# Last layer's expert results added in memory: tokens stored behind the attention, scatters that accumulate, rows copied from memory to the output

## The chip, the cores and the metric

The kernel runs on one core of one Trainium2 chip, in one launch. The metric is the time of one execution on the device in microseconds (us); of several executions the median is taken. Engines are called PE (matrix multiplication), DVE (vector), ACT (scalar), POOL (GpSimd) and SP (the engine that here only issues transfers). A view of the profile always belongs to one profiled execution.

## The reference

The input `x` has 16 x 256 tokens of 128 channels, all in float32. Four residual layers follow one another, each on a layer norm of `x`:

```python
x = x + attn_a(layernorm(x))      # 16 heads of 8, in blocks of 64 tokens of a sequence
x = x + ffn(layernorm(x))         # mixture of experts
x = x + attn_b(layernorm(x))      # 16 heads, over the 16 sequences, with a bias
x = x + ffn(layernorm(x))         # the same experts and the same router weights
```

The mixture of experts chooses two of eight experts for every token:

```python
logits = flat_x @ Wr
top_vals, top_idx = top_k(logits, 2)
rw = softmax(top_vals)
h  = silu(flat_x @ Wg[e]) * (flat_x @ Wu[e])         # hidden size 512
out = sum over the two experts e of  rw_e * (h @ Wd[e]) / sqrt(12)
```

So every one of the 4096 tokens gets two expert rows, and the final output is the token after `attn_b` plus these two rows.

## The kernel before

The tokens stay on the chip in four tiles `xq[q]`, one for each quarter of the 256 positions: 128 partitions x 8 groups x 128 channels, 1024 tokens a quarter.

**Experts by lists of tiles.** A router (`router(layer, q)`) finds each token's two experts and scatters the token's normalised row twice into a memory tensor `sorted_in[layer]`, where every expert has a region. A row there carries the 128 channels, its weight in column C, and in column C + 1 the place where its result is to go. `tile_tables` then cuts the regions into tiles of 256 rows: 39 tiles a layer, in three lists of 9, 8 and 22. The first list is known after two quarters, the second after three, the third after all four. An expert tile is two *units* of work in `experts(layer)`: its rows (`xin`, L861) and its expert's weights (`w`, three loads of 256 KB, L877 to L879) are fetched by SP two tiles ahead into three buffers; PE multiplies by `wg` and `wu` (L947), ACT and DVE form `h` (L952 to L955), PE multiplies by `wd` (L897) and turns the result back (L908), and ACT scales it into `yo` (L913; six buffers). Then POOL scatters the 256 rows by two indirect DMAs of 128 rows each (L920) into `results[layer]`, to the places in `to`. Where the last list's tiles overlap rows done before, `to` points to padding rows behind the results.

**Combination.** `results[layer]` has two rows for every token, so all scatters of a layer go to different rows and are not ordered among each other. `combine(layer, part)` loads the pairs of half a quarter (`back`, L973, 512 KB), waiting for the scatters of all tiles that can hold rows of that quarter (`READY`: 24, 24, 31 and 39 tiles), and DVE adds the two rows to `xq` (L983). In layer 1 two further DMAs store the half quarter from `xq` to the output (L986).

**Order of the work.** The program text sets the order: `weave` takes steps of one generator between those of another. Layer 0's expert tiles run beside `attn_b` of the quarters before; `begin_b(q)` combines layer 0's results for quarter q and prepares its attention, `finish_b(q)` multiplies by the output weights and adds to `xq[q]` (L580). After the third quarter's `finish_b`, `begin_b` of the fourth runs beside the first four tiles of layer 1. The layer's first tiles run beside the attention and the router of the fourth quarter; the rest run alone, up to `BEGIN[q]` units, each time followed by the combination of a quarter. Every engine works through its own instructions in order, and SP's and POOL's DMA issues are part of that: an issue that waits holds up what stands behind it. Inside the framework an order of small pieces can be moved by its scheduler, so the order of each engine's instructions is read from the built program.

`declare_no_dep`, `add_to_no_dep_group` and `follow` tell the framework which accesses to a memory tensor are independent, and which waits are set by hand.

Of the kernel before, what the change touches and what calls it, by code (L numbers as in the profile page):

```python
# [64 lines left out]
K_PAD = K_DEST + TOP * NQ * NG  # L65
K_ROW = K_PAD + 2 * KMAX
K_FIRST = K_ROW + 2
K_END = K_FIRST + NE

B_Q, B_K, B_TOR, B_IQ, B_IK, B_IV = range(6)  # L70

# [1 line left out]
def _constants():  # L73
    p = np.arange(P)[:, None]
    h = np.arange(H)[None, :]
    c = np.zeros((P, K_END), np.float32)
    c[:, K_ID : K_ID + P] = np.eye(P)

    c[:, K_HM : K_HM + 4] = (p // D) % 4 == np.arange(4)[None, :]

    c[:, K_PM : K_PM + H] = p // 64 == h % 2
    c[:, K_M4 : K_M4 + H] = p // 32 == h % 4

    eye = np.eye(S)
# [19 lines left out]
    c[:, K_ROW : K_ROW + 2] = 2 * p + np.arange(2)  # L104

    c[:, K_FIRST : K_FIRST + NE] = NTOK * np.arange(NE)
    return c
# [3 lines left out]
def hybrid_kernel(  # L111
# [111 lines left out]
        nc.gpsimd.memset(t[:, 0:NG], 0.0)  # L223


    sorted_in = [dram.tile([NE * NTOK, RW], F32, name=f"sorted_in{i}") for i in range(2)]
    results = [dram.tile([TOP * NTOK + KMAX * TT, C], F32, name=f"results{i}") for i in range(2)]

    zero = const.tile([P, TT // P * RW], F32, name="zero")
    nc.gpsimd.memset(zero, 0.0)  # L230
# [354 lines left out]
    def router(layer, q):  # L585
# [12 lines left out]
        for g in range(NG):  # L598
# [253 lines left out]
    def experts(layer):  # L852
# [41 lines left out]
        def down(li, i, t, w, elsewhere, acc, pair, h):  # L894
# [7 lines left out]
            if pair == 1:  # L902
# [13 lines left out]
                    )  # L916
                to = p6.tile([P, 2], I32, tag="to", name=f"to_{n}")
                nc.vector.tensor_tensor(to, t[:, :, C + 1], elsewhere, ALU.max)
                for b in range(2):
                    put_row = nc.gpsimd.indirect_dma_start(  # L920
                        out=results[layer],
# [5 lines left out]
                    key = f"result_{layer}"  # L927
                    tc.declare_no_dep(put_row.ins, group=key, reason="rows of different places")
                    tc.add_to_no_dep_group(key, put_row.ins)
                    puts.setdefault(layer, []).append(put_row.ins)  # L930
# [35 lines left out]
        yield  # L966


    def combine(layer, part):
        q, gs = part // 2, slice(4 * (part % 2), 4 * (part % 2) + 4)  # L970
        rows_of = slice(part * 4 * P * TOP, (part + 1) * 4 * P * TOP)
        t = p2.tile([P, 4, TOP, C], F32, tag="back", name=f"back_{layer}_{part}")
        got = nc.sync.dma_start(  # L973
            out=t.rearrange("p g k c -> p g (k c)"),
            in_=results[layer][rows_of].rearrange("(g p k) c -> p g (k c)", p=P, k=TOP),
        )
        known = puts[layer][: 2 * READY[q]]
        key = f"result_{layer}"
        tc.declare_no_dep(got.ins, group=key, keep=known, reason="rows of tiles done before")
        tc.add_to_no_dep_group(key, got.ins)  # L980
        follow(got.ins, known)
        for k in range(TOP):
            nc.vector.tensor_tensor(xq[q][:, gs], xq[q][:, gs], t[:, :, k], ALU.add)  # L983
        if layer == 1:
            for s2 in range(2):
                nc.sync.dma_start(  # L986
                    out=out.rearrange("(g s) t c -> s t g c", s=2)[
                        s2, q * BS : (q + 1) * BS, gs
                    ],
                    in_=xq[q][s2 * BS : (s2 + 1) * BS, gs, :],  # L990
                )

# [34 lines left out]

    def begin_b(q):  # L1030
        for part in range(2 * q, 2 * q + 2):
            combine(0, part)
            yield
        yield from normal_b(q)
        yield from prepare_b(q, 0)
# [7 lines left out]
    for layer in range(2):  # L1043
# [10 lines left out]
        for q in range(NQ):  # L1054
            for half in range(2):
# [78 lines left out]
```

## Time and profile before

| | us |
|---|---|
| median of 3 runs | 983.16 |
| lowest and highest run | 980.27, 992.81 |
| the profiled execution | 1056.63 |
| its span, first to last instruction | 1054.9 |

| engine | busy us | share of the span |
|---|---|---|
| PE | 901.1 | 85% |
| DVE | 619.6 | 59% |
| ACT | 397.6 | 38% |
| POOL | 361.1 | 34% |

The profiled execution is longer than the timed ones, so shares of it are carried over rather than differences. The mean granted PE clock of it is 0.911.

How to read the lines: in a timeline, the columns are the start in us from the span's beginning, the duration in us, engine, line, operation, output <- inputs, the count, and in brackets how long the engine was idle before it and what ended that. In the chain of waits, each line is start, duration and what the end of the run was waiting for at that time. In a list of waits, it is who waited for whom, us in total, times, and the longest. In the groups of the page, it is line, engine, operation, output <- inputs, count, busy us, mean ns, and idle time before with what ended most of it.

### The profile page before, as it was taken

To read this page: it belongs to the slowest core of one execution; us is meant where nothing else is said; L and a number is where in the kernel's file an instruction comes from. 1 tells how busy PE (TensorE), PEld (TensorE's weight loads), DVE (VectorE), ACT (ScalarE), POOL (GpSimd) and SP (SyncE) were. 2 spreads that over 40 slices of the span, in tenths; PEclk is the share of its full clock that TensorE was granted. 3 is DMA by queue.
4 is the path that set the end of the run, shared out by engine and by line. 5 is a ranking of instruction groups with operands and counts; after the bars stand their busy time and mean duration, and the time that the engine had idled before them with its cause. 6 is when DMAs were issued, how large, how long until landed. Compare 5 with 4: busy or idle time off the path is not lost.

```text
span 1054.9 us, 17640 instructions
## 1 busy us (share of the span) xinstructions
PE 901.1 (85%) x5992; PEld 733.6 (70%) x5992; DVE 619.6 (59%) x1749; ACT 397.6 (38%) x773; POOL 361.1 (34%) x404
## 2 busy tenths in 40 slices
PE   5987897989989979989887789588976997999993
PEld 3765666768778758877765667467765776887872
DVE  4676357557746745577766447546754674456452
ACT  2442243244434323436444254233622332443431
POOL 2121522442443463341112631442225345333322
PEclk9997787689989999999997889898978988999997
DMA  7000000041333545673121211133203444568772
GB/s 198 3 2 1 29 14 1 21 127 41 99 101 106 151 149 166 196 225 96 42 81 41 65 58 42 61 95 127 81 14 109 121 134 148 170 192 253 222 213 88
DMA packets 104922, 107.69 MB, mean 102 GB/s; under 512 B 10688, under 2 KB 80320, under 8 KB 104832
## 3 DMA queue, kind: packets, MB, share of 16 engines
q1 hardware_dynamic: 95024, 87.36, 27.8%
q0 software_dynamic: 9088, 18.89, 5.1%
q8 instruction: 48, 0.79, 0.3%
q10 hardware_dynamic: 720, 0.30, 0.1%
q14 instruction: 42, 0.34, 0.1%
HBM read 83.38 MB, written 23.13 MB: 101 GB/s over the span
## 4 chain that ended last, share of the span: by engine, by line
PE 66%; DVE 12%; DMA 6%; another core or an unknown queue 5%; ACT 5%; issue 4%; POOL 1%; SPq 1%; ACTq 0%; POOLq 0%; DVEq 0%
PE g L947 11%; PE acc L897 10%; PE u L947 10%; PE o_A L441 6%; PE sc_A L411 6%; PE t_A L430 3%; PE v_B L354 3%; PE o_B L554 2%; DMA back<-results 2%; PE sc_B L517 2%; DMA xin<-sorted_in 2%; DMA results<-yo,to 2%; PE v_A L354 2%; PE lg_F L599 1%
## 5 line engine op out<-in xcount | busy, mean ns | idle before, releaser
L920 POOL DMA_INDIRECT results<-yo,to x156 | 154.1, 988 | 299.7 <-ACT yo L913 269.3
L897 PE MATMUL acc<-h,w 128*128 128x256 f32 x624 | 174.3, 401 | 12.1 <-DVE h L955 9.1
L947 PE MATMUL g<-xT,w 128*128 128x256 f32 x624 | 171.5, 394 | 4.4 <-issue 2.7
L947 PE MATMUL u<-xT,w 128*128 128x256 f32 x624 | 169.8, 393 | 3.8 <-DVE th L953 2.0
L952 ACT ACTIVATE th<-g 128x512 f32<-128x512 f32 x156 | 93.6, 600 | 203.8 <-PE g L947 132.1
L953 DVE SCALAR_TENSOR_TENSOR th<-th,g 128x512 f32<-128x512 f32 x156 | 106.4, 683 | 105.6 <-ACT th L952 84.0
L694 POOL DMA_INDIRECT sorted_in<-rows,pos_i_F x128 | 125.0, 977 | 124.7 <-issue 38.4
L897 PEld LDWEIGHTS acc<-h,w 128*128 128x128 f32 x624 | 121.6, 200 | 36.4 <-DVE h L955 14.8
L947 PEld LDWEIGHTS g<-xT,w 128*128 128x128 f32 x624 | 119.0, 198 | 23.0 <-issue 4.9
L947 PEld LDWEIGHTS u<-xT,w 128*128 128x128 f32 x624 | 115.7, 196 | 20.4 <-issue 3.4
L955 DVE TENSOR_TENSOR h<-th,u 128x512 f32<-128x512 f32 x156 | 106.6, 684 | 21.6 <-remote 5.6
L411 PE MATMUL sc_A<-k_A,q_A 128*128 128x256 f32 x256 | 86.4, 456 | 19.0 <-DVE ex_A L420 14.1
L441 PEld LDWEIGHTS o_A<-va,eT_A 128*64 128x64 f32 x1024 | 63.6, 147 | 20.4 <-issue 8.4
L411 PEld LDWEIGHTS sc_A<-k_A,q_A 128*128 128x128 f32 x256 | 50.8, 225 | 33.2 <-DVE ex_A L420 16.3
L441 PE MATMUL o_A<-va,eT_A 128*64 128x18 f32 x1024 | 67.7, 219 | 5.6 <-issue 3.1
L905 ACT COPY yT<-acc 128x256 f32<-128x256 f32 x78 | 29.0, 372 | 100.6 <-PE acc L897 89.2
L419 DVE TENSOR_REDUCE mx_A<-sc_A 128x8 f32<-128x512 f32 x64 | 43.1, 681 | 35.5 <-PE sc_A L411 34.8
L434 ACT COPY eT_A<-t_A 128x512 f32<-128x512 f32 x64 | 36.6, 589 | 67.9 <-PE t_A L430 61.8
L449 POOL TENSOR_TENSOR xq<-xq,att_A 128x128 f32<-128x128 f32 x32 | 14.6, 456 | 130.5 <-DVE att_A L373 120.1
L913 ACT ACTIVATE yo<-y,xin 128x128 f32<-128x128 f32 x156 | 48.6, 366 | 20.4 <-PE y L908 10.6
L425 ACT ACTIVATE ex_A<-ex_A 128x1024 f32<-128x1024 f32 x32 | 34.0, 1064 | 42.5 <-DVE ex_A L420 31.0
L430 PEld LDWEIGHTS t_A<-k_sb,ex_A 128*128 128x128 f32 x256 | 34.0, 159 | 20.7 <-issue 10.4
(173 smaller groups left out, 1318.0 us busy)
## 6 DMA issues: line engine op xcount, KB each, us to landing
w<-in_wg SPq DMA_DIRECT2D x78, 256.0 KB
w<-in_wu SPq DMA_DIRECT2D x78, 256.0 KB
w<-in_wd SPq DMA_DIRECT2D x78, 256.0 KB
xin<-sorted_in SPq DMA_DIRECT2D x78, 132.0 KB
back<-results SPq DMA_DIRECT2D x16, 512.0 KB
results<-yo,to POOLq DMA_INDIRECT x156
sorted_in<-zero SPq DMA_DIRECT2D x2, 1056.0 KB
sorted_in<-rows,pos_i_F POOLq DMA_INDIRECT x128
```

Source lines behind the costliest of these rows:

```text
L354: nc.tensor.matmul(pv[:, a * P : (a + 1) * P], lhsT=src[:, g * n + a].rearrange("p r k -> p (r k)"), rhs=w, start=True, stop=True,)
L411: nc.tensor.matmul(sc[:, v * 4 * BS : (v + 1) * 4 * BS], lhsT=qT[:, blk, 2 * v : 2 * v + 2, :].rearrange("p r k -> p (r k)"), rhs=kx[:, :, ...
L430: nc.tensor.transpose(pt[:, i * P : (i + 1) * P], ex[:, b, 2 * i : 2 * i + 2, :].rearrange("p h k -> p (h k)"), ident,)
L441: nc.tensor.matmul(po[b * BS : (b + 1) * BS, i * 18 : (i + 1) * 18], lhsT=eT[:, b, 2 * v + i % 2, u * BS : (u + 1) * BS], rhs=vt[:, b, 2 * ...
L694: put_row = nc.gpsimd.indirect_dma_start(out=sorted_in[layer], out_offset=bass.IndirectOffsetOnAxis(ap=pos_i[:, k, g : g + 1], axis=0), in ...
L897: nc.tensor.matmul(acc[:, 0:TT], lhsT=w[:, 2, hc * P : (hc + 1) * P], rhs=h[:, j * TT : (j + 1) * TT], start=(hc == 0), stop=(hc == NHC - 1),)
L913: nc.scalar.activation(y[:, b, :], py[:, b * P : (b + 1) * P], AF.Identity, scale=t[:, b, C : C + 1],)
L920: put_row = nc.gpsimd.indirect_dma_start(out=results[layer], out_offset=bass.IndirectOffsetOnAxis(ap=to[:, b : b + 1], axis=0), in_=y[:, b ...
L947: nc.tensor.matmul(p[:, j * TT : (j + 1) * TT], lhsT=w[:, k, hs], rhs=xT, start=True, stop=True,)
L952: nc.scalar.activation(th, pg, AF.Tanh, scale=0.5)
L953: nc.vector.scalar_tensor_tensor(th, th, 1.0, pg, ALU.add, ALU.mult)
L955: beat[0] = nc.vector.tensor_tensor(h, th, pu, ALU.mult).ins
```

## The change

Only layer 1, the last, is treated differently; layer 0 keeps the combination described above.

- `results[1]`'s first 4096 rows become `sums`: one row for every token. After `finish_b(q)`, `store(q)` stores `xq[q]` (512 KB) there, from SP.
- The router writes a token's own place, the same for both of its rows, into column C + 1 (a new block of constants, `K_PLACE`).
- The tiles' scatters of layer 1 get `compute_op` add: the DMA adds the rows to what is in memory. As two tiles can hold rows of the same token, each pair of scatters waits for the pair before (`puts[...][-2:]`), and for the stores of the quarters that its list knows.
- `leave(q)` takes the place of `combine(1, part)`: two DMAs from SP, memory to memory, 256 KB each, copy a quarter's rows from `sums` to the output. There is no load of `back`, no addition on DVE and no store from `xq` in this layer any more.

```diff
+    sums = results[1][0:NTOK]
...
-        nc.gpsimd.tensor_copy(
-            row[:, :, :, C + 1],
-            const_of(at, TOP * NG).rearrange("p (g k) -> p g k", k=TOP),
-        )
+        place = const_of(at, TOP * NG).rearrange("p (g k) -> p g k", k=TOP)
+        if layer == 1:
+            place = const_of(K_PLACE + q * NG, NG).unsqueeze(2).to_broadcast([P, NG, TOP])
+        nc.gpsimd.tensor_copy(row[:, :, :, C + 1], place)
...
+                key, done = f"result_{layer}", []
+                if layer == 1:
+                    done = stores[: LISTED + li] + puts.get(layer, [])[-2:]
                 for b in range(2):
                     put_row = nc.gpsimd.indirect_dma_start(
...
                         in_=y[:, b, :], in_offset=None,
+                        **({} if layer == 0 else {"compute_op": ALU.add}),
+                    ).ins
+                    tc.declare_no_dep(
+                        put_row, group=key, keep=done, reason="rows of different places"
                     )
...
+                    follow(put_row, done)
...
-        if layer == 1:
-            for s2 in range(2):
-                nc.sync.dma_start(
-                    out=out.rearrange("(g s) t c -> s t g c", s=2)[
-                        s2, q * BS : (q + 1) * BS, gs
-                    ],
-                    in_=xq[q][s2 * BS : (s2 + 1) * BS, gs, :],
-                )
+    def store(q):
+        put = nc.sync.dma_start(
+            out=sums[q * TQ : (q + 1) * TQ].rearrange("(g p) c -> p g c", p=P), in_=xq[q]
+        ).ins
+        tc.declare_no_dep(put, group="result_1", reason="rows of other quarters")
+        tc.add_to_no_dep_group("result_1", put)
+        stores.append(put)
+
+    def leave(q):
+        for s2 in range(2):
+            got = nc.sync.dma_start(
+                out=out.rearrange("(g s) t c -> s g t c", s=2)[s2, :, q * BS : (q + 1) * BS],
+                in_=sums[q * TQ : (q + 1) * TQ].rearrange(
+                    "(g s t) c -> s g t c", s=2, t=BS
+                )[s2],
+            )
+            by_known(got.ins, 1, q)
...
                 if layer == 1 and half == 1:
                     finish_b(q)
+                    store(q)
...
     for q in range(NQ):
         run(units(1, BEGIN[q]))
-        for part in range(2 * q, 2 * q + 2):
-            combine(1, part)
+        leave(q)
```

`by_known(ins, layer, q)` makes a transfer wait for the scatters of the first `READY[q]` tiles, as `combine` did before.

More of the change, by code (lines that the diff above doesn't have):

```diff
@@ L67 @@
 K_FIRST = K_ROW + 2
-K_END = K_FIRST + NE
+K_PLACE = K_FIRST + NE
+K_END = K_PLACE + NQ * NG
 B_Q, B_K, B_TOR, B_IQ, B_IK, B_IV = range(6)
@@ L104, in _constants @@
     c[:, K_ROW : K_ROW + 2] = 2 * p + np.arange(2)
+    c[:, K_PLACE : K_PLACE + NQ * NG] = place[:, :, 0]
     c[:, K_FIRST : K_FIRST + NE] = NTOK * np.arange(NE)
@@ L925, in down @@
                         in_=y[:, b, :], in_offset=None,
-                    )
[L927 to L930, printed above, removed]
+                        **({} if layer == 0 else {"compute_op": ALU.add}),
+                    ).ins
+                    tc.declare_no_dep(
+                        put_row, group=key, keep=done, reason="rows of different places"
+                    )
+                    tc.add_to_no_dep_group(key, put_row)
+                    follow(put_row, done)
+                    puts.setdefault(layer, []).append(put_row)
         todo = [(li, i) for li, k in enumerate(LISTS) for i in range(k)]
@@ L966, in experts, with combine @@
         yield
-    def combine(layer, part):
+    def combine(part):
         q, gs = part // 2, slice(4 * (part % 2), 4 * (part % 2) + 4)
         rows_of = slice(part * 4 * P * TOP, (part + 1) * 4 * P * TOP)
-        t = p2.tile([P, 4, TOP, C], F32, tag="back", name=f"back_{layer}_{part}")
+        t = p2.tile([P, 4, TOP, C], F32, tag="back", name=f"back_{part}")
         got = nc.sync.dma_start(
             out=t.rearrange("p g k c -> p g (k c)"),
-            in_=results[layer][rows_of].rearrange("(g p k) c -> p g (k c)", p=P, k=TOP),
+            in_=results[0][rows_of].rearrange("(g p k) c -> p g (k c)", p=P, k=TOP),
@@ L976, in combine, with by_known @@
         )
+        by_known(got.ins, 0, q)
+        for k in range(TOP):
+            nc.vector.tensor_tensor(xq[q][:, gs], xq[q][:, gs], t[:, :, k], ALU.add)
+    def by_known(ins, layer, q):
         known = puts[layer][: 2 * READY[q]]
         key = f"result_{layer}"
[L979 to L983, printed above, removed]
@@ L984, in combine @@
-        if layer == 1:
-            for s2 in range(2):
-                nc.sync.dma_start(
-                    out=out.rearrange("(g s) t c -> s t g c", s=2)[
-                        s2, q * BS : (q + 1) * BS, gs
-                    ],
-                    in_=xq[q][s2 * BS : (s2 + 1) * BS, gs, :],
-                )
+        tc.declare_no_dep(ins, group=key, keep=known, reason="rows of tiles done before")
+        tc.add_to_no_dep_group(key, ins)
+        follow(ins, known)
+    stores = []
@@ L1031, in begin_b @@
         for part in range(2 * q, 2 * q + 2):
-            combine(0, part)
+            combine(part)
             yield
```

## The prediction

> **What bounds the kernel now.** I read four views in this order: the page's head and costliest groups, the chain of waits at the end of the run, the timelines of POOL and SP over the last 150 us, and SP's waits. First, how large the scatters are and what they wait for:
>
> ```profile
> span 1054.9 us, 17640 instructions
> PE 901.1 (85%) x5992; PEld 733.6 (70%) x5992; DVE 619.6 (59%) x1749; ACT 397.6 (38%) x773; POOL 361.1 (34%) x404
> L920 POOL DMA_INDIRECT results<-yo,to x156 | 154.1, 988 | 299.7 <-ACT yo L913 269.3
> ```
>
> PE is the fullest engine. POOL issues 156 scatters, two for each of the 78 expert tiles, and waits mostly for ScalarE's `yo`, not for memory. Now POOL's timeline in the stage where only expert tiles are left:
>
> ```profile
> 943.32 0.96 POOL L920 DMA_INDIRECT results<-yo,to  x1 [3.39 <-ACT yo L913]
> 944.58 0.96 POOL L920 DMA_INDIRECT results<-yo,to  x1 [0.30 <-DVE h L955]
> 948.94 0.96 POOL L920 DMA_INDIRECT results<-yo,to  x1 [3.40 <-ACT yo L913]
> 950.20 0.96 POOL L920 DMA_INDIRECT results<-yo,to  x1 [0.30 <-DVE h L955]
> ```
>
> The reader should see a pair every 5.62 us (948.94 - 943.32), with the second scatter 1.26 us after the first. PE sets 5.62: in the slices from 898 to 943 us PE is busy 45.0 of 45.0 us at clock 1.00. The chain of waits then shows what interrupts this pace and what ends the run:
>
> ```profile
> 950.20 3.35 DMA results<-yo,to
> 954.26 5.01 DMA back<-results
> 964.58 4.66 DMA xin<-sorted_in
> ...
> 994.07 3.43 DMA results<-yo,to
> 999.22 5.84 DMA xin<-sorted_in
> ...
> 1041.12 2.24 DMA results<-yo,to
> 1043.55 4.07 DMA back<-results
> ```
>
> A plain scatter lands 3.35 to 3.43 us after its issue begins while weights are being loaded, and 2.24 us after it when they are not. Two places are lost to the combination: around 954 and 999 us, where SP, which issues in order, waits for scatters, loads `back`, waits for DVE and only then fetches the next `xin`; and the tail, 1043.4 to 1054.9, 11.5 us. SP's own waits say the same:
>
> ```profile
> SPq L973 <- DMA results<-yo,to: 27.4, 7, 13.7
> SPq L986 <- DVE xq L983: 10.9, 6, 4.6
> ```
>
> [...] The trace of before has no accumulating DMA and no copy from memory to memory, [...] it only shows the plain 2.24 to 3.43 us.
>
> **The change part by part**, against the profiled execution (span 1054.9, whole execution 1056.63; the median of the three timed runs is 983.16, 7% less, so I carry the result over as a share).
>
> 1. *Removed stalls.* Counting POOL's pairs, tile 14 of the layer (from 0) starts its scatter at 898.37 and tile 38, the last, at 1039.85: 141.5 us for 24 intervals. At 5.62 they would take 134.9; the last is 1.8 shorter, since no next tile is interleaved. So 141.5 - 134.9 + 1.8 = 8.4 us go to the two interruptions. With `leave` SP waits for the scatters alone, no longer for DVE, and issues four (then two) copies. The order of after puts the first copy where the first `back` stood and the others behind the next tile's weights. They are 256 KB each[...]. I leave 2 us of stall: gain 6.4.
>
> 2. *Removed tail.* Before, 11.5 us: `back` load, four adds of 0.69 us, four `out` issues, landing. After: reaction 0.2, two issues (about 0.9, as the two `back` issues took), and two copies side by side.[...] Sum 5.6, gain 5.9; bounds 4 to 9 us for the tail.
>
> 3. *Removed adds.* 16 adds of 0.69 us on DVE (11 us). Outside the tail DVE is 59% busy and PE rules, so nothing beyond 1 and 2.
>
> 4. *Added stores.* Four 512 KB stores on SP, each waiting for finish_b's last DVE add. Three cost nothing, as SP is idle there: the adds end at 553.0, 640.7 and 833.7 us and the fetches behind them are issued at 575.07, 645.87 and 837.54. The third does not: the order puts it ahead of the two `back` loads of the last quarter.
>
> ```profile
> 714.66 0.93 SPq L973 DMA_DIRECT2D back<-results  x2
> 715.01 0.69 DVE L580 TENSOR_TENSOR xq<-y_B,xq 128x512 f32<-128x512 f32 x1 [3.12 <-PE y_B L574]
> 716.60 0.69 DVE L580 TENSOR_TENSOR xq<-y_B,xq 128x512 f32<-128x512 f32 x1 [0.90 <-PE y_B L574]
> 721.59 0.68 DVE L983 TENSOR_TENSOR xq<-xq,back 128x512 f32<-128x512 f32 x1
> ```
>
> The store can go at 717.3 + 0.3, `back` at about 718.1 instead of 714.66: 3.4 later, and its packets queue behind the store's. Behind `back` stand the next fetch, the layer norm of the last quarter and PE's transposes (PE works in order). DVE was a little late there, so not all of it passes through: I take 3 us, bounds 0 to 6. POOL's order also moves the first `rs_B` behind a scatter pair (2.5 us); it is ready that late anyway by then.
>
> 5. *Scatters that add.* Each pair waits for the landing of the one before. The period of that chain is: first issue to second 1.26, landing 3.4, reaction 0.1, together 4.76 us for plain writes. Adding raises it twice.[...] I take 0.2 for each of the two scatters[...]. Landing:[...] I take 1.0[...], because weights load all the time. Period: 4.76 + 0.4 + 1.0 = 6.16 us[...]. While POOL waits, nothing else of use is queued behind it in this stage; ScalarE can run six tiles ahead (`yo` has six buffers). Earlier, between 850 and 895 us, two to four other scatters of 1.27 us stand between pairs, so the landing is covered there[...].
>
> So the chain, not PE, sets the pace: 24 x 6.16 = 147.8 us from 898.4 gives 1046.2 for the last pair's start. It then lags PE by about two tiles, whose landings find no weights loading (2.24 instead of 3.4): -2.4. Landing of the last pair: 1.26 + 0.2 + 2.24 + 0.2 + 1.0 = 4.9. That is 1048.7; the tail of 5.6 gives 1054.3, the store 3 us: 1057.3 against 1054.9, +0.2%. The stalls removed in 1 don't count here, as a chain that lags absorbs them. On 983.16: 985 us.
>
> **Rivals.**
> A, *PE stays the bound* (period at most 5.62[...]). For it: the data of a scatter are only 64 KB, and POOL has 3.4 us of slack in each tile. Against: that slack is nearly all landing time. Then: -6.4 - 5.9 + 3 + 1.2 for the last landing = -8 us, -0.8%: 976. With no store or copy cost it could be -1.4%: 970.
>
> B, *slower: the landing of adding scatters is the bound by far*. One mechanism, in POOL's chain from tile 14 on; its price is 24 us for each us of period. It passes 2% (21 us) where the period exceeds 6.95, that is, where adding costs more than 2.2 us a pair over plain writes.[...]
>
> C, *the gain is swallowed elsewhere*: PE bound as in A, but the copies[...] delay `xin` at three places by 4 us each. Then -8 + 12 = +4, +0.4%: 987. It looks like my forecast in time but shows PE waiting on `xin`, not POOL on scatters.
>
> **How the numbers follow.** My case 0.37, A 0.25, B 0.30, C 0.08. Predicted 985. A's best is 970 and B's worst[...] over 1020; I take 971 to 1020. Two per cent is about what a measurement of this kernel can tell from no change. Faster by more would need 20 us, and all that the combination costs after 898 us is 8.4 + 5.9: 0.02. B alone is slower by more: 0.30. The rest: 0.68.
>
> **What would show it.** Right: POOL's pairs 6.0 to 6.4 us apart from about tile 14 on, each waiting for a scatter and no longer for `yo`; landings of about 4.6 us; a tail of about 5.6 us after the last landing; `back` for the last quarter 3 to 5 us later after finish_b. Wrong: pairs at 5.62 still waiting for `yo` (A); a period over 7 or POOL instructions well over 1.2 us (B); PE waiting on `xin` (C).

## The result, and the profile after

The changed kernel takes 1025.3 us (median of 4 runs, 1023.83 to 1028.89), the kernel before 982.08 (4 runs, 980.27 to 992.81): ratio 1.0469, interval 1.0421 to 1.0517. The forecast of 985 us was wrong, and so was its range of 971 to 1020. Every ratio in this document is of each kernel's fast executions alone (those within 1.5% of its fastest), so it can differ from the quotient of two medians, and the profiled executions of e8 and f1 are not among the fast ones.

One thing must be known to read the numbers. The groups of experiments ran on four chips: on one of them the kernel before takes 983 us (median), on the other three 1045 to 1054. I call these a chip of 982 and chips of 1050. The timed runs behave like the first. The profile of before that the prediction worked with (1056.63 us) looks like the others; which chip it came from is not on record. The execution profiled after the change is one of the timed ones (1024.74 us), so I compare it with a second profile of before, from the chip of 982 (e1, one execution, span 976.0). First the pages' heads, before (e1) and after:

```profile
span 976.0 us, 17640 instructions
PE 858.6 (88%) x5992; PEld 707.0 (72%) x5992; DVE 620.8 (64%) x1749; ACT 397.1 (41%) x773; POOL 359.9 (37%) x404
q0 software_dynamic: 9088, 18.89, 5.5%
L920 POOL DMA_INDIRECT results<-yo,to x156 | 152.9, 980 | 268.4 <-ACT yo L913 236.4
```

```profile
span 1023.0 us, 17603 instructions
PE 879.5 (86%) x5992; PEld 722.9 (71%) x5992; DVE 612.6 (60%) x1733; ACT 397.0 (39%) x773; POOL 405.1 (40%) x404
q0 software_dynamic: 17824, 18.89, 9.0%
L930 POOL DMA_INDIRECT results<-yo,to x156 | 197.8, 1268 | 290.9 <-ACT yo L918 178.3
```

The scatter queue q0 moves the same 18.89 MB in twice the packets. Each of the 78 adding scatters now has 128 packets of one row instead of 16 packets of eight rows: 78 x 112 = 8736 more. POOL is busy 45 us longer with the same number of instructions (the mean of 1268 ns mixes layer 0's 0.96 us with layer 1's 1.54). PE, too, is busy 21 us longer with the same 5992 matmuls. I had not looked for that.

POOL's timeline where only expert tiles are left, before (e1) and then after, answers the lines shown in the prediction:

```profile
848.35 0.96 POOL L920 DMA_INDIRECT results<-yo,to  x1 [3.40 <-ACT yo L913]
849.62 0.96 POOL L920 DMA_INDIRECT results<-yo,to  x1 [0.31 <-DVE h L955]
853.97 0.96 POOL L920 DMA_INDIRECT results<-yo,to  x1 [3.40 <-ACT yo L913]
```

```profile
920.14 1.54 POOL L930 DMA_INDIRECT results<-yo,to  x1 [4.45 <-ACT yo L918]
921.99 1.54 POOL L930 DMA_INDIRECT results<-yo,to  x1 [0.30 <-issue]
929.32 1.54 POOL L930 DMA_INDIRECT results<-yo,to  x1 [5.79 <-ACT yo L918]
931.16 1.54 POOL L930 DMA_INDIRECT results<-yo,to  x1 [0.30 <-ACT xT L896]
937.40 1.54 POOL L930 DMA_INDIRECT results<-yo,to  x1 [4.70 <-ACT th L965]
...
1005.74 1.54 POOL L930 DMA_INDIRECT results<-yo,to  x1 [2.40 <-DMA results<-yo,to]
1007.58 1.54 POOL L930 DMA_INDIRECT results<-yo,to  x1 [0.30 <-issue]
1011.50 1.54 POOL L930 DMA_INDIRECT results<-yo,to  x1 [2.38 <-DMA results<-yo,to]
```

A pair came every 5.62 us; now it is 9.18 and 8.08 us in the first stretch and 5.76 at the end, when no weights are loading. The releaser named in the brackets is not always the true one (`th`, `xT` and `yo` had often been done for long). The DMA packets in the trace show it: in 21 of the 24 intervals from tile 14 to 38 the next pair starts 1.0 to 1.2 us after the last packet of the pair before, whatever the bracket names. The chain of waits names the landing at the end of the run, and shows what lies between it and the next pair:

```profile
1007.58 3.16 DMA results<-yo,to
1010.81 0.69 issue
1011.50 1.54 POOL results L930
```

So the shortest possible period is 1.84 (first issue to second) + 3.16 (landing, from the start of the second issue) + 0.76 (1011.50 - 1010.74) = 5.76 us. That is above PE's 5.62 even here, where no other packet moves while the pair lands. Over the 24 intervals the three terms are 1.84, 4.1 and 0.8 us on average: the landing is the one that stretches, from 3.2 to 6.6 us. (These are worked out from the packets; the last packet ends 0.35 us before the landing that the chain shows.)

The ledger, from the starts of the first scatters of the last layer's tiles 0, 1, 14 and 38:

| stretch, us | before (e1) | after | difference |
|---|---|---|---|
| start to tile 0 | 684.5 | 684.9 | +0.4 |
| tile 0 to 1 | 8.4 | 14.2 | +5.9 |
| tile 1 to 14 (beside attention and router) | 128.7 | 150.0 | +21.3 |
| tile 14 to 38 (tiles alone) | 139.3 | 162.4 | +23.0 |
| tile 38 to the end | 15.1 | 11.5 | -3.6 |
| span | 976.0 | 1023.0 | +47.0 |

The table by stage of the two profiles of that chip, e1 and then after, and of the recorded profile of before. The columns are the window, its length, busy time of PE, PE's weight loads, DVE, ACT and POOL (with instructions), granted clock, DMA share and GB/s:

```profile
693.00:822.00 129.00, 123.03 (x899) 103.08 (x900) 94.74 (x303) 57.67 (x120) 63.46 (x65) 1.00 0.42 124
822.00:961.00 139.00, 129.52 (x635) 111.14 (x633) 73.21 (x126) 54.60 (x139) 46.01 (x49) 1.00 0.68 204
```

```profile
699.00:849.00 150.00, 136.22 (x913) 113.34 (x912) 98.58 (x308) 59.32 (x125) 79.31 (x64) 0.91 0.48 118
849.00:1011.00 162.00, 132.79 (x622) 112.52 (x621) 63.31 (x109) 53.18 (x134) 73.97 (x48) 0.91 0.62 148
```

```profile
738.00:898.00 160.00, 134.51 (x878) 110.25 (x877) 93.93 (x301) 56.29 (x116) 63.84 (x64) 0.88 0.33 100
```

In the stage beside the attention 13.2 of the 21.3 us are PE itself running longer, at clock 0.91 instead of 1.00; the rest is PE standing still (13.8 us instead of 6.0). The trace has PE's clock at half for 27.3 us of this stage, in stretches of 3.4, 3.4, 13.7 and 6.8 us, and half of 27.3 is about the 13.2. In the recorded profile of before that stage had 0.88 and 134.5 us of PE already.

At two places after the change a wait on POOL is followed by a gap on PE, and the gap goes with half its clock. The first: POOL, then PE, then three windows of 3 us:

```profile
779.34 1.57 POOL L930 DMA_INDIRECT results<-yo,to  x1 [3.86 <-ACT th L965]
781.21 1.55 POOL L930 DMA_INDIRECT results<-yo,to  x1 [0.30 <-issue]
782.21 1.64 POOL L284 TENSOR_TENSOR rs_F<-ve_F,minus_half 128x4 f32<-128x4 f32 x1
```

```profile
784.38 1.29 PE L304 MATMUL lnp_F<-k_sb,rows 128*128 128x128 f32 x4 [3.24 <-DVE mv_F L280]
786.27 1.16 PE L304 MATMUL lnp_F<-k_sb,rows 128*128 128x128 f32 x4 [0.60 <-DVE rows L291]
787.55 2.07 PE L960 MATMUL u<-xT,w 128*128 128x256 f32 x4
...
798.74 1.03 PE L960 MATMUL g<-xT,w 128*128 128x256 f32 x4
```

```profile
783.00:786.00 3.00, 1.29 (x4) 0.73 (x4) 1.47 (x7) 0.29 (x1) 1.89 (x2) 0.69 1.01 252
792.00:795.00 3.00, 3.00 (x10) 2.55 (x11) 1.56 (x7) 0.00 (x0) 0.00 (x0) 0.50 0.00 0
798.00:801.00 3.00, 3.00 (x18) 2.40 (x16) 2.79 (x14) 1.68 (x6) 0.07 (x1) 1.00 0.01 3
```

The pair at 779.34 waits 3.86 us for the pair before to land; the router's `rs_F` stands behind both in POOL's queue, DVE can form the rows only after it, and PE waits 3.24 us for them (`mv_F` in the bracket is not the cause). Then the same four matmuls take 2.07 us instead of 1.03. In e1 PE stands still at this place for 1.4 us in all (771 to 777), at a clock of 1.00.

The second place ends the stage. The router's last scatter, behind the adding pairs in POOL's queue, is issued at 840.21. The rows of the third list can be fetched only when it has landed, and PE waits for them. The chain of waits, then PE:

```profile
840.21 2.30 DMA sorted_in<-rows,pos_i_F
842.71 2.43 DMA xin<-sorted_in
```

```profile
845.18 0.69 PE L894 MATMUL xt<-k_sb,xin 128*128 128x128 f32 x2 [5.02 <-DMA xin<-sorted_in]
```

In e1 the router's last scatter is issued at 817.83, and PE does not wait for `xin` in this stage.

Four gaps of PE after the change (3.24 and 5.02 us here, 10.78 and 6.00 us where it waits for `xin` in the stage of tiles alone) each go with a stretch at half clock (0.50) that begins 2.0 to 3.6 us after the gap does and lasts 6.8 or 13.7 us. At the first place PE worked for about 11 us without a pause before the clock came back. Gaps do not account for every stretch: the two of 3.4 us (at 729.5 and 746.5) follow no gap above 1.3 us. In the 30 us that hold both (721.7 to 751.7) PE stands still for 4.0 us in all; in e1, around the same work (714 to 744), it stands still for 4.4 us, with the clock at 1.00. Why is open.

### The profile page after: what moved, and what is told of

Its sections match the earlier page's. It is cut to its first block, busy times and chain, and to the rows that moved or that the text cites. A ratio compares the mean times of both kernels' runs of the same rounds, so it can differ in the third digit from the quotient of the medians.

```text
span 1023.0 us, 17603 instructions
## 1 busy us (share of the span) xinstructions
PE 879.5 (86%) x5992; PEld 722.9 (71%) x5992; DVE 612.6 (60%) x1733; ACT 397.0 (39%) x773; POOL 405.1 (40%) x404
## 3 DMA queue, kind: packets, MB, share of 16 engines
q0 software_dynamic: 17824, 18.89, 9.0%
## 5 line engine op out<-in xcount | busy, mean ns | idle before, releaser
L930 POOL DMA_INDIRECT results<-yo,to x156 | 197.8, 1268 | 290.9 <-ACT yo L918 178.3
L902 PE MATMUL acc<-h,w 128*128 128x256 f32 x624 | 167.5, 389 | 4.4 <-DVE h L968 4.2
L902 PEld LDWEIGHTS acc<-h,w 128*128 128x128 f32 x624 | 118.4, 195 | 26.3 <-DVE h L968 9.5
L416 PE MATMUL sc_A<-k_A,q_A 128*128 128x256 f32 x256 | 83.3, 442 | 19.1 <-DVE ex_A L425 14.1
L894 PE MATMUL xt<-k_sb,xin 128*128 128x128 f32 x156 | 31.9, 288 | 31.3 <-DMA xin<-sorted_in 24.1
```

The source lines that it names most:

```text
L416: nc.tensor.matmul(sc[:, v * 4 * BS : (v + 1) * 4 * BS], lhsT=qT[:, blk, 2 * v : 2 * v + 2, :].rearrange("p r k -> p (r k)"), rhs=kx[:, :, ...
L894: nc.tensor.transpose(pt[:, b * P : (b + 1) * P], t[:, b, 0:C], ident)
L902: nc.tensor.matmul(acc[:, 0:TT], lhsT=w[:, 2, hc * P : (hc + 1) * P], rhs=h[:, j * TT : (j + 1) * TT], start=(hc == 0), stop=(hc == NHC - 1),)
L930: put_row = nc.gpsimd.indirect_dma_start(out=results[layer], out_offset=bass.IndirectOffsetOnAxis(ap=to[:, b : b + 1], axis=0), in_=y[:, b ...
```

## Experiments

My theory after the result was: the wait of each pair for the landing of the pair just before sets the pace, with single-row packets that queue among the weights' packets. Rivals were the longer issue alone, the stores, and SP, which waits at the copies with the next `xin` behind it. The ratios below are to the kernel before on the same chip. The quotient of the medians differs from the ratio by up to 0.8% (e3: 1.0056 and 1.0130), so smaller differences between totals are not read. The stages are those of the ledger, in us, from one profiled execution each; three profiles of the unchanged kernel after differ by 5 us in the first and 2 us in the second.

| run | ratio (interval) | tile 1 to 14 | tile 14 to 38 |
|---|---|---|---|
| chip of 982: before (e1) | | 128.7 | 139.3 |
| after | 1.0469 (1.0421 to 1.0517) | 150.0 | 162.4 |
| e2 plain writes | 1.0000 (0.9974 to 1.0026) | 130.5 | 137.4 |
| e3 add, no wait | 1.0130 (1.0040 to 1.0219) | 135.6 | 137.6 |
| e4 no stores | 1.0493 (1.0402 to 1.0585) | 153.3 | 163.6 |
| chips of 1050: before (recorded profile) | | 160.8 | 141.5 |
| after (e9) | 1.0215 (1.0106 to 1.0324) | 158.6 | 163.3 |
| after (f3) | 1.0211 (1.0149 to 1.0273) | 162.3 | 164.3 |
| after (g2) | 1.0239 (1.0182 to 1.0296) | 157.0 | 162.0 |
| e5 copies last | 1.0183 (1.0096 to 1.0269) | 161.8 | 159.5 |
| e6 copies on POOL | 1.0195 (1.0113 to 1.0277) | 159.4 | 160.3 |
| e7 add late | 1.0208 (1.0145 to 1.0271) | 154.4 | 161.9 |
| e12 add late | 1.0249 (1.0166 to 1.0332) | 158.1 | 163.8 |
| g3 add late | 1.0197 (1.0133 to 1.0262) | 157.0 | 163.6 |
| e8 before, combination spread | 1.0033 (0.9983 to 1.0083) | 157.0 | 141.1 |
| e10 no weights | 1.0107 (1.0008 to 1.0206) | 159.0 | 150.5 |
| e11 two sums | 0.9874 (0.9832 to 0.9916) | 153.8 | 134.3 |
| f2 two sums | 0.9937 (0.9905 to 0.9969) | 153.7 | 137.1 |
| f1 two sums, whole | 1.0050 (1.0022 to 1.0078) | 156.7 | 143.8 |
| g1 router's norm off POOL | 1.0176 (1.0123 to 1.0228) | 156.0 | 161.7 |

### e1: before again

The kernel before, unchanged, for a profile on a chip of 982.

> The kernel before, once more, for a profile of an execution whose time is near the timed ones (982 us; the profiled one shown above took 1056.63). If the loss of 43 us lies in the stage from tile 14 on alone, tile 14 should start its scatter near 849 us, as in the changed kernel; if part of it lies earlier, tile 14 should start near 823 us, since from there to the end the recorded profile of before took 156.5 us.

977.75 us, span 976.0, tile 14 at 821.62. It gave the ledger above: 27 of the 47 us are lost before tile 14, where the prediction had put about 4 (an estimate: 1 for the longer issue, 3 for the store).

### e2: the waits without the add

```diff
-                        **({} if layer == 0 else {"compute_op": ALU.add}),
```

> The changed kernel with plain writes in place of the adding ones (the sums are left out), all waits kept. Theory 1, the add makes the chain slow: the chain's period falls to 1.27 + 3.4 + 0.1 = 4.8 us, under PE's 5.62, pairs stand 5.62 us apart, POOL's scatter takes 0.96 us again, and the time is 972 to 985 us. Theory 2, waiting for the pair before is what costs, with whatever kind of write: the time stays at 1010 us or more and pairs stay over 6 us apart.

978.32 us, ratio 1.0000. The wait for the pair before, the stores and the copies are all in this kernel, and together they cost no more than they save. A plain write lands early enough for the chain to fit under PE's period, though not by as much as the expectation has it: with the landing of 3.4 us on average and a reaction of 0.8 the chain needs 5.5 us, not 4.8. So the order alone costs nothing; it takes the add to make it cost.

### e3: the add without the waits

Every row is added to a place of its own, which starts at zero; no pair waits for another. The tokens and the copies live in another tensor, so the experts' results are left out of the output.

```diff
-    sums = results[1][0:NTOK]
+    held = dram.tile([NTOK, C], F32, name="held")
+    sums = held
...
-                    done = stores[: LISTED + li] + puts.get(layer, [])[-2:]
+                    done = []
```

> Adding scatters that go to places of their own (two rows for a token, zeroed at the start), so that no pair waits for another; the stores and the final copies stay, in a tensor of their own, and the two rows are never added to the token. Theory 1a, the serial wait together with the longer landing is the cost: pairs 5.62 us apart, about 980 to 990 us. Theory 1b, the longer issue of an adding scatter (1.54 us against 0.96) on POOL is the cost: it stays on POOL in front of the router's scatters, and the time is 1005 us or more.

988.57 us, ratio 1.0130: 6 to 13 us more than before, by the medians or by the ratio, and 10 more than the plain writes of e2. This is what the longer issue and the many packets cost by themselves, and nearly all of it shows before tile 14. The rest, 33 to 37 us, needs the wait for the landing. From tile 14 on the adds without waits take 137.6 us, no more than the kernel before.

### e4: no stores

```diff
-                    store(q)
```

The sums start at zero instead; the tokens are left out of the output.

> The changed kernel without the four stores of the tokens (the sums start from zeros written at the start, so the tokens are left out of the output); adds, waits and copies kept. If the store ahead of the last quarter's back loads costs what the prediction said: 3 us less, about 1022 us. If the stores are the reason for the loss before tile 14: 15 to 25 us less, 1000 to 1010 us.

Tile 0 to 1 falls from 14.24 to 10.05 us, so the third store costs about 4.2 us where it stands. (In the profile of e4 everything up to tile 0 is 6 us later, so tile 1 doesn't start earlier. But e2, with stores and plain writes, agrees: 12.4 us there against 8.4 in e1.) The total doesn't fall (1026.5 us, with runs from 1021 to 1032). That the 4 us are lost again in the stages behind, which a chain of landings paces, is my reading.

### e5 and e6: the copies out of SP's way

e5 writes the copies behind the last tile (the call of `leave` moved below the loop); e6 issues them from POOL.

```diff
-            got = nc.sync.dma_start(
+            got = nc.gpsimd.dma_start(
```

> The changed kernel with all four quarters' copies to the output issued after the last tile, so that SP never waits for scatters while tiles are to be fetched; everything else as in the changed kernel. Theory 1, SP's wait for a lagging chain starves PE, and PE then starves the chain: the 24 intervals from tile 14 to 38 shrink from 162.4 us to about 24 x 5.9 = 142, the tail grows by 3 to 6 us for four quarters' copies, the stretch before tile 14 stays, and the time is 1007 to 1013 us. Theory 2, the chain alone is that slow when weights are loading: the 24 intervals stay above 155 us and the time is 1022 us or more.

> The changed kernel with the copies to the output issued by POOL instead of SP, at the same places. POOL has waited for the pair before anyway, so a copy waits for nothing more. Theory 1 (SP's wait is the cost of the stage): 24 intervals in about 145 us, three of them longer by POOL's issue of the copies; 1005 to 1012 us. Theory 2: over 155 us and 1020 us or more.

e5 was inconclusive: the framework's scheduler moved the copies back between the tiles, and SP waited at them for 49.9 us in all (54.2 in the profile after). In e6 SP no longer waits there:

```profile
POOL results L930 <- DMA results<-yo,to: 32.5, 11, 4.7
PE xt L894 <- DMA xin<-sorted_in: 3.5, 2, 3.4
```

PE's wait for `xin` from tile 14 on is 3.5 us instead of 16.8 in the profile after and 17.0 in e9, and still the stage takes 160.3 us. SP's wait is real, but without it the stage is only 2 to 4 us shorter, and the tail with copies issued by POOL is 3 us longer (14.7 us): the chain of landings would have taken most of that time anyway.

### e7, e12, g3: adding only from tile 14 on

```diff
-                        **({} if layer == 0 else {"compute_op": ALU.add}),
+                        **({} if layer == 0 or len(puts.get(1, [])) < 2 * 14 else {"compute_op": ALU.add}),
```

> The changed kernel with plain writes for the first 14 tiles of the layer and adding ones from tile 14 on (the sums of the first tiles are wrong), all waits kept. If what is lost before tile 14 comes from the add's longer issue and landing on POOL in front of the router's work: the stretch from tile 1 to 14 falls from 150.0 to 130.5 us as with plain writes throughout, the 24 intervals after it stay near 162, and the time is about 1005 us. If it comes from the waits or the stores alone: 1020 us or more.

> The first 14 tiles of the last layer write plainly instead of adding (their sums are then not whole); the waits stay. Beside the changed kernel on the same chip it shows what the adds of the stage beside the attention cost the total. Theory 'about half of the loss arises there': on a chip of 982 us 17 to 24 us less than the changed kernel, ratio 1.02 to 1.03; on a chip of 1050 us 2 to 8 us less. Rival 'what is lost there is made up later, since the chain lags anyway': less than 5 us on any chip.

> Plain writes for the first 14 tiles of the last layer, the waits stay (their sums are not whole). On a chip of about 982 us: 14 to 22 us less than the changed kernel if the adds of that stage cost what the ledger says (tile 1 to 14 at about 131 us), less than 5 if the chain regains it later. On a chip of about 1050 us: within 5 us of the changed kernel, as twice before.

All three ran on chips of 1050: 1073.45, 1077.23 and 1072.29 us, against 1073.48 and 1076.86 for the changed kernel beside the second and the third. Taking the adds out of the stage beside the attention gains nothing clear of the spread there (3.7 us more and 4.6 us less). In the recorded profile of before DVE, ACT and PE already stand still together at two places of that stage (PE for 4.9 and 4.6 us), waiting for something that the profile can't name, and the mean clock is already 0.88. What it gains on the chip of 982 was not tried; e2, with plain writes throughout, has 130.5 us in that stage.

### e8: the kernel before with its combination spread

The load of `back`, the adds and the output stores of a quarter stand one tile apart each (the second quarter's start three tiles later), to take the stalls out of the kernel before without adding in memory.

> The kernel before, its last combination taken apart: the load of back, DVE's adds and the stores to the output are put one tile (two units) after one another, with the next tile's fetch between them; plain scatters, no accumulation in memory. If the 8 us of PE's stalls around the combination come from SP waiting for back and for DVE ahead of the fetches, they go: 24 intervals from tile 14 to 38 in about 131 to 133 us instead of 139.3, and about 975 us (ratio 0.992). If the stalls come from the traffic of the combination itself, they stay, and so does the time.

1052.93 us, ratio 1.0033: no gain. The stalls remain (intervals of 7.6, 9.5 and 7.9 us). But the edit did not take SP's waits away: from tile 14 on SP waits 20.8 us for scatters and 10.1 for DVE, 20.7 and 10.9 in the recorded profile of before. So the run does not decide between the two causes in its expectation.

### e9, f3, g2: the changed kernel on other chips

> The changed kernel again, for the chip of this group. Both theories: the share lost against the kernel before depends on the chip's clock. On a chip where before takes about 982 us: ratio 1.04 to 1.05. On one where before takes about 1050 us, TensorE is slower beside the attention and hides part of the waits of that stage: ratio 1.02 to 1.03. From the layer's tile 14 to tile 38: 161 to 164 us on either.

> The changed kernel on the chip of this group. If the chip's clock decides: ratio 1.042 to 1.052 where before takes about 982 us, 1.015 to 1.03 where it takes about 1050 us. If the two earlier ratios differed for another reason, this one falls elsewhere.

> The changed kernel for the chip of this group: ratio 1.042 to 1.052 where before takes about 982 us, 1.015 to 1.03 where it takes about 1050.

1073.48, 1068.32 and 1076.86 us, ratios 1.0211 to 1.0239. The stage of tiles alone costs the same on all chips (162 to 164 us against 139 to 141). What differs is tile 1 to 14: +21 us on the chip of 982, and no loss on the others, within their spread (157 to 162, against 160.8 in the recorded profile and 157.0 in e8).

### e10: no weights from tile 14 on

```diff
+            at = sum(LISTS[:li]) + i
+            if layer == 1 and at >= 14:
+                return t, last_w[0], no_pads if behind is None else behind[:, i]
```

> The last layer's tiles from the 14th on keep the weights of the tile before and load none; their results are therefore other numbers, everything else runs as in the change. Theory 'weights' packets stretch the landing': the pairs from tile 14 on stand at the unloaded period, 5.75 to 5.9 us, so the 24 intervals take 138 to 143 us instead of 163, and the whole falls by 18 to 25 us. Rival 'the wait on the copies and the fetches behind them makes the long intervals, or the adding itself is slow': the landings keep their length, the 24 intervals stay above 155 us and the whole falls by less than 8 us.

The 24 intervals fall from 163.3 to 150.5 us, less than the 138 to 143 expected and more than the rival allowed. The whole is 1065.75 us, 7.7 less than the changed kernel beside it, but the intervals of the two ratios overlap. Both theories hold in part. Nine of the first ten intervals are 5.8 to 6.05 us, one is 7.05; the eleventh is the last one here:

```profile
936.54 1.54 POOL L936 DMA_INDIRECT results<-yo,to  x1 [2.54 <-ACT xT L902]
938.39 1.54 POOL L936 DMA_INDIRECT results<-yo,to  x1 [0.30 <-ACT th L971]
942.37 1.54 POOL L936 DMA_INDIRECT results<-yo,to  x1 [2.44 <-ACT xT L902]
...
961.17 1.54 POOL L936 DMA_INDIRECT results<-yo,to  x1 [2.51 <-ACT yT L916]
963.02 1.54 POOL L936 DMA_INDIRECT results<-yo,to  x1 [0.30 <-issue]
971.35 1.54 POOL L936 DMA_INDIRECT results<-yo,to  x1 [6.79 <-DVE th L972]
```

The pair at 961.17 meets the copies to the output (1.1 MB moved while it lands) and the next one stands 10.18 us later: its last packet ends 7.0 us after its second issue begins, against 2.9 to 3.0 for the pairs on either side. So other transfers stretch the landing, the weights by about 13 us in the stage. With the weights gone, the landings of the 24 intervals still exceed the unloaded one by 11 us in all, 4 of them at the pair shown.

### e11 and f2: two sums

Odd tiles add into a second tensor, so that a pair waits for the pair two before it. The second tensor starts at zero and is left out of the output.

```diff
-                    done = stores[: LISTED + li] + puts.get(layer, [])[-2:]
+                    done = stores[: LISTED + li] + puts.get(layer, [])[-4:-2]
...
-                        out=results[layer],
+                        out=second if layer == 1 and len(puts.get(1, [])) % 4 >= 2 else results[layer],
```

> Odd tiles add into a second tensor that starts at zero, so a pair waits for the pair two before it, not one; what the odd tiles add is left out of the output. Theory 'the landing of the pair just before stands in the chain': that landing then has a whole tile's time, the wait is nearly never last, the 24 intervals take 137 to 142 us, tile 1 to 14 about 135 us as without waits, the whole is within 2 us of the kernel without pair waits: ratio 1.01 to 1.02 on a chip of 982 us. Rival 'two adds to memory disturb each other however far apart, or the number of packets is the cost': the intervals stay above 155 us, ratio above 1.035.

> Two sums, the odd tiles' left out of the output, once more for the chip of this group. On a chip of about 982 us the question is the stage from tile 1 to 14. If the wait for the pair just before costs there: about 133 to 138 us (150.0 with the change), total ratio 1.005 to 1.015. If the longer issue of adding scatters costs there: 145 us or more, ratio above 1.02. On a chip of about 1050 us: ratio 0.98 to 0.995 again.

f2's timeline from tile 14 on, and its waits there (us in total, times, longest):

```profile
921.78 1.54 POOL L937 DMA_INDIRECT results<-yo,to  x1 [2.23 <-ACT yo L925]
923.62 1.54 POOL L937 DMA_INDIRECT results<-yo,to  x1 [0.30 <-issue]
927.39 1.54 POOL L937 DMA_INDIRECT second<-yo,to  x1 [2.23 <-ACT yo L925]
```

```profile
POOL results L937 <- ACT yo L925: 28.5, 12, 5.2
POOL second L937 <- ACT yo L925: 26.9, 11, 5.2
```

The period is 5.61 us again and nearly every pair waits for `yo`: the same number of adds, packets and weights, and the 162 to 164 us are 134.3 and 137.1. The whole is 1044.92 us against 1073.48 for the changed kernel on its chip, and 1038.70 against 1068.32: 29 and 30 us less in the medians. With e3 this settles the stage of tiles alone: the cost is the wait for the pair just before, and nothing else of the adding. Both runs fell on chips of 1050, so the stage before tile 14 on the chip of 982 stays without this test.

### f1: two sums, and both in the output

SP copies the odd sum to the output and POOL adds the even sum to it with an accumulating transfer from memory to memory.

```diff
+    def complete(q):
+        for s2 in range(2):
+            got = nc.gpsimd.dma_start(
...
+                accum_op=ALU.add, max_dma_last_dim=8192,
+            )
```

> The two sums with nothing left out: SP copies the odd tiles' sum to the output, and POOL then adds the even tiles' sum to it by an accumulating transfer in pieces of 8 KB, two issues for each quarter. Theory 'only the wait for the pair just before costs': the intervals stay near those of the two sums without it, 134 to 142 us from tile 14 to 38, and the end grows by one accumulating transfer of 2 x 256 KB in place of a copy: estimate 3 to 6 us more than the copy's 6.4. On a chip where before takes about 1050 us: ratio 0.99 to 0.995; on one of 982 us: 1.01 to 1.02. Rival 'the transfers that POOL issues and waits for stop the scatters behind them': intervals above 150 us, ratio above 1.015 on any chip.

1054.52 us, ratio 1.0050. The changed kernel's loss goes from 2.1% to 0.5%, but it does not beat the kernel before; e11 and f2, which are faster, leave the odd tiles' results out. The end shows the price:

```profile
1036.36 1.54 POOL L937 DMA_INDIRECT results<-yo,to  x1 [0.42 <-ACT yo L925]
1038.20 1.54 POOL L937 DMA_INDIRECT results<-yo,to  x1 [0.30 <-issue]
1043.87 1.86 POOL L1036 DMA_DIRECT2D out_x<-results  x2 [4.13 <-DMA results<-yo,to]
```

From the accumulating transfers' issue at 1043.87 to the end of the span at 1055.1 are 11.2 us, against 6.3 for the plain copies after the change (which SP issues). The accumulating packets move for 5.2 of them (1045.4 to 1050.6), the plain ones for 3.3; of the rest, 4.5 us stand between the last packet and the end, 1.6 with the plain copies. The earlier ones stand in POOL's queue between the pairs; that stage takes 143.8 us instead of 137.1.

### g1: the router's norm off POOL

```diff
+            if name.startswith("F"):
+                nc.vector.tensor_copy(rstd[:, some], veps)
+            else:
+                nc.gpsimd.tensor_tensor(rstd[:, some], veps, minus_half[:, some], ALU.pow)
```

> The changed kernel with the router's rs_F as a copy on VectorE instead of a power on POOL (the power is left out: the tokens' scale into the router and the experts is another number, the choice of experts the same). Theory 'rs_F behind a waiting pair opens a gap on PE, after which its clock is halved for some 12 us': on a chip where before takes about 982 us the gap of 3.2 us around the last router and the 0.50 after it vanish, PE's clock in the stage from tile 1 to 14 rises, that stage falls by 6 to 11 us from 150, the whole by 4 to 11. Rival 'the chain of pairs has lost that time anyway': the stage keeps 147 us or more, the whole falls by less than 3. On a chip of about 1050 us, where such gaps are there before the change too: less than 4 us either way.

1071.12 us against 1076.86 for the changed kernel beside it; the intervals of the two ratios overlap. It ran on a chip of 1050, where PE's gap behind the last `rs_F` is 0.77 us with and without the edit, so it says nothing on the 3.24 us of the other chip. That the gaps and the halved clock make up the 13 us of PE there is read from the trace and not shown by an experiment. Why the chips differ stays open too.

## Why the prediction was wrong

*Step 5, the period.* The prediction had 6.16 us; the mean of the 24 intervals is 162.4 / 24 = 6.77. The order of things was right: the chain, not PE, sets the pace from tile 14 on. The term that failed is the reaction from a landing to the next pair's issue. The prediction put it at 0.1 without a source; it is 0.76 unloaded and 0.8 on average. The other two terms missed as well, in opposite directions:

| term of the period, us | predicted | measured, mean of 24 |
|---|---|---|
| first issue to second | 1.46 | 1.84 |
| landing | 4.6 | 4.1 |
| reaction | 0.1 | 0.8 |
| period | 6.16 | 6.77 |

The profile of before has no adding scatter, so the 0.2 us for each issue and the 1.0 us for the landing were estimates of mine, resting on no trace. The issue of an adding scatter is 0.58 us longer (1.54 against 0.96). Beyond the issue, the landing grew by less than the 1.0: with nothing beside it, it went from 2.24 to 3.16, and 0.58 of this is the issue, which leaves 0.34. That the overestimate of the landing hid part of the other two errors was luck. The deduction of 2.4 us for the last landings was right in kind: the last three intervals are 5.81, 5.79 and 5.76 us. The 24 intervals should then have taken 147.8 - 2.4 = 145.4 us; they took 17 more.

*Step 5, before tile 14.* That "the landing is covered there", with about 1 us more for the issues, was the largest error on the chip of the result: the stage took 21.3 us more. It fails in the wait and in the path. What stands between the pairs are the router's scatters and `rs_F`, and they wait behind each pair that waits. I named what is queued behind the waiting instruction for the last stage only. Of the difference to the plain writes of e2 (130.5 us), e3 puts about 5 us on the longer issue and the many packets (135.6), and the change against e3 about 14 on the wait (150.0).

*The carrying over as a share.* On chips of 1050 the loss is 2.1 to 2.4%, nearly all of it from tile 14 on; in the timed runs it is 4.7%. The recorded profile held PE gaps of 4.9 and 4.6 us and stretches at half clock beside the attention (mean 0.88) that e1 does not have (1.00). A profile 7% longer than the runs was a warning that a share doesn't carry.

*Steps 1 to 3.* The stalls removed were indeed swallowed by the chain. e11 and f2 show what they would have been worth: their copies still cost 5.0 us of longer intervals, where the prediction left 2, so the gain is about 3.4 of the 8.4 us and not 6.4. (The rest of their lead over the recorded 141.5 us comes from a late tile 14 that the next tiles catch up with.) The tail was nearly right: 5.6 us predicted, of which 4.5 for the two copies were an estimate of mine, and 6.5 measured from the last landing to the end.

*Step 4.* Right in size, about 4 us measured for 3 predicted, and `back` did queue behind the store (in the profile after the store's packets of 512 bytes run from 676.3 to 678.6 us, `back`'s of 1024 bytes from 678.3 to 682.2). But its part of the sum was wrong: in e4 removing it gains nothing that four runs can tell.

*The rivals.* B is nearest to what happened, but not for its reason alone. Its signs were a period over 7 us or POOL instructions well over 1.2: the instructions take 1.54, the period is 6.77, and the landing, which B blamed, is on average shorter than in my own case. At that period, B's price of 24 us for each us gives 15 us more than my case. The rest of the loss on the chip of 982 is the stage before tile 14, which B had left out, so the end of the range, 1020 us, which was my estimate of B's worst, was still too low. A, PE as the bound, is what e11 and f2 show from tile 14 on once the wait is two pairs back. C's sign, PE waiting on `xin`, was there (16.8 us) and cost little, as e6 shows.

## What to carry to other kernels

Adds into memory that are made to wait for one another turn independent scatters into a chain. Its period is issue + landing + reaction, each read under load (here 1.84 + 4.1 + 0.8 us), and it must fit under the tile's period (here 5.62 us); waiting for the pair two before instead of one took away 29 to 30 us here. No term may be set near zero without a trace: the 0.1 us of reaction was 0.8. Where an instruction gets a wait, list what is queued behind it in every stage, not only in the last. Look at PE's clock around every gap that this opens: the four longest in the stages compared each went with 6.8 or 13.7 us at half clock. When the profiled execution is several per cent longer than the timed ones, look for the stage that makes the difference before a sum is carried over.

## What the hardware showed that I had not expected

- An indirect scatter of 128 rows of 512 bytes was issued by POOL in 0.96 us when it writes (e1) and in 1.54 us when it adds (after). Writing, it moved as packets of 4096 bytes (0.17 us each); adding, every row was a packet of its own (512 bytes, 0.08 us).
- The landing of a pair that adds changed with what moved beside it: its last packet ends 2.8 us after the second issue begins when nothing else moves (after), and 7.0 us after it while 1.1 MB of other transfers, the copies among them, pass (e10).
- From the landing that it waits for to its next scatter POOL took 0.76 us (after), where two scatters that wait for nothing stood 0.30 us apart.
- A gap of 3.24 us on PE went with half its clock for 13.7 us, from 3.0 us after its start. Two other stretches at half clock, of 3.4 us each, follow no such gap.
- Accumulating 2 x 256 KB from memory to memory, issued by POOL in pieces of 8 KB, took 11.2 us from issue to the end of the kernel, with packets moving for 5.2 of them; a plain copy of the same size, issued by SP in packets of 32 KB, took 6.3, with packets moving for 3.3.
